# A four-layer graph block on Trainium2: attention's output product from twelve-bit parts in every step, with the transposes in one group and the next block's scores behind the mix

## The chip, the cores and the metric

The kernel runs on one core of a Trainium2 chip. The metric is the device time of one execution in microseconds (us), the median of repeated runs; lower is better. All times below are of this kernel on this chip. PE is the matrix engine, PEld its weight loads, DVE the vector engine, ACT the scalar engine, POOL the GpSimd engine, SP the queue that issues most transfers.

## The reference

`x` holds 1024 nodes by 512 features. After a normalisation and a first graph convolution, four layers follow, and then a second graph convolution and two residual sums. Per layer:

```python
def _attn(xf, cond, Wq, Wk, Wv, Wo):            # BS, M, H, DH = 16, 256, 8, 64
    xb = xf.reshape(BS, n // BS, d)             # 16 batches of 64 nodes
    q = (xb @ Wq).reshape(BS, -1, H, DH)
    k = (cond @ Wk).reshape(BS, -1, H, DH)      # cond: 16 x 256 x 512
    v = (cond @ Wv).reshape(BS, -1, H, DH)
    att = jnp.einsum('bnhd,bmhd->bhnm', q, k) * DH ** (-0.5)
    w = jax.nn.softmax(att, axis=-1)
    o = jnp.einsum('bhnm,bmhd->bnhd', w, v).reshape(BS, -1, H * DH)
    return (o @ Wo).reshape(n, d)
...
for i in range(L):                              # L = 4
    h = h + _attn(_ln(h, ln2_w[i], ln2_b[i]), cond, Wq[i], Wk[i], Wv[i], Wo[i])
    u = _ln(h, ln3_w[i], ln3_b[i]) @ geglu_w[i] + geglu_b[i]
    val, gate = jnp.split(u, 2, axis=-1)
    h = h + (val * jax.nn.gelu(gate, approximate=False)) @ ffo_w[i] + ffo_b[i]
```

The product that the change rewrites is `o @ Wo`, 1024x512 by 512x512, once per layer.

## The kernel before, in words

`h` lives in eight tiles of 128 rows, h[0] to h[7] (`hall` in the trace). Block g holds two batches of 64 nodes. The attention of a layer is a loop over g (L1580 onwards); in **step g** the keys and values of block g+1 are made while the softmax of block g is finished and weighed with its values.

**Twelve-bit products.** Keys and values come from class `Twelve` (L338 to L384). An operand x is cut into a high part (ACT, L314), a low part (DVE, L315) and a third part, high minus low (POOL, L320, in four pieces `as_c` of 128x512 per block). `begin` multiplies high by high and low by low, 4 matmuls of 128x512 each in the fp32r type (L366), and ACT scales the bank in place (L377). `end` adds third by third on top, 4 matmuls, and copies the bank out (DVE L382 or ACT L384). So PE cannot start a unit's `end` before ACT has done that unit's L377. Four units make the keys k_0 to k_3 of a block and four the values v_0 to v_3.

**Softmax.** `scores` issues 32 matmuls (L835), four row maxima on DVE (L842, `nmax`), eight exponentials on ACT (L847) and on DVE four reciprocals and eight scalings (L850, L852). In step g it stands at the head of the step, between v_2's and v_3's `end` of block g. `mix` transposes the four probability tiles on PE (`tr_pr`, L201), copies them out as `pT` (ACT L886 and DVE L884, in turn), and multiplies them with the values, 64 small matmuls into the bank `po` (L870). Between the second and third transposed tile and behind the fourth it calls hooks, in which k_3's `end` and v_0's `begin` are multiplied. DVE copies `po` to `oT` (L893).

**Output product.** Blocks 0 to 5 go by pairs: in every odd step `pair_sums` makes sums of the two `oT` on POOL (L919 to L922) and `attn_out_pair` makes seven products of 2 x 128x256 matmuls per bank half (through `multiply`, L297; tiles `oab`, `ocd`) in plain fp32, spread between the value units and the next step's scores, with sums on DVE and POOL. The right-hand sums `wo_sums` are made once a layer on POOL (L909). Blocks 6 and 7 go alone through `attn_out` (L899, `pw`, plain fp32), in a tail in which the first products of the feed-forward part (`ga`, class `Quad`, L297) fill PE.

**Order.** PE's order is that of the code, held by `pin`. DVE, ACT and POOL are in-order queues, filled by a scheduler that keeps to the readiness it models unless `in_order`, `waiting_for` or `issue_after` say otherwise. In odd steps `split_cond`, which cuts the operand for the block after next, stood behind `pair_sums` by `tc.issue_after`. The base of the last residual sum (`x_again`, `bias_out`) is fetched and added in steps 1 and 2 of each layer (L1557, L1558).

Of the kernel before, what the change touches and what calls it, by code (L numbers as in the profile page):

```python
# [17 lines left out]
P = 128  # L18
# [7 lines left out]
def gnn_kernel(  # L26
# [82 lines left out]
    def bank(name):  # L109
        return psum.tile([P, 512], F32, tag="bank", name=name)  # L110
# [746 lines left out]
    def mix(l, g, probs, v, hooks, each=pin):  # L857

        oT = t512(f"oT_{l}_{g}")
        po = bank(f"po_{l}_{g}")  # L860
# [16 lines left out]
        for c2 in range(2):  # L877
            pTs = []
            for j in range(2):
                u = 2 * c2 + j  # L880
                pt = transposed(probs[u], f"pr_{l}_{g}_{u}", each)
                pT = t512(f"pT_{l}_{g}_{u}")
                if j:
                    nc.vector.tensor_copy(pT, pt)  # L884
# [8 lines left out]
        mix.last = nc.vector.tensor_copy(oT, po)  # L893
        return oT

    def attn_out(l, g, oT, wo):
        pw = bank(f"pw_{l}_{g}")
        for c in range(HP):
            nc.tensor.matmul(pw, oT[:, c * P:(c + 1) * P], wo[c // 2][:, c % 2, :],  # L899
                             start=(c == 0), stop=(c == HP - 1))  # L900
        nc.vector.tensor_tensor(h[g], pw, h[g], OP.add)

    def wo_sums(wo):

        b11, b12, b21, b22 = (wo[k][:, :, d * M:(d + 1) * M] for k in range(2) for d in range(2))
        sums = four_wide("wo_sums")
        t1, t2, t3, t4 = (halves_of(sums[:, i, :]) for i in range(4))
        for to, of, less in ((t1, b12, b11), (t3, b22, b12), (t2, b22, t1), (t4, b21, t2)):
            nc.gpsimd.tensor_tensor(to, of, less, OP.subtract)  # L909
        return [b11, b21, b22, t4, t1, t2, t3]  # L910

    def pair_sums(l, g, oTs):

        n = f"{l}_{g}"
        t = nc.gpsimd
        a11, a12, a21, a22 = (halves_of(oT[:, k * M:(k + 1) * M]) for oT in oTs for k in range(2))
        s, more = acc_tile(f"os_{n}"), acc_tile(f"om_{n}")
        s1, s2, s4 = (halves_of(x) for x in (s[:, :M], s[:, M:], more[:, :M]))
        t.tensor_tensor(s1, a21, a22, OP.add)  # L919
        t.tensor_tensor(a21, a11, a21, OP.subtract)  # L920
        t.tensor_tensor(s2, s1, a11, OP.subtract)
        pair_sums.last = t.tensor_tensor(s4, a12, s2, OP.subtract)  # L922
        return [a11, a12, s4, a22, s1, s2, a21], more[:, M:], acc_tile(f"ou_{n}")

    def attn_out_pair(g, left, p1, kept, right, ab, cd, each=lambda ins: ins):


        t = nc.gpsimd
        a, b, c, d = ab[:, :M], ab[:, M:], cd[:, :M], cd[:, M:]
        h11, h12, h21, h22 = (h[g + i][:, j * M:(j + 1) * M] for i in range(2) for j in range(2))  # L930

        def product(i, to, start):
            multiply(to, left[i], right[i], [(0, P, 0, M)], start, each)

        u2, p7 = kept[:, :M], kept[:, M:]
        product(0, a, True)
        nc.scalar.copy(p1, a)
        product(6, c, True)
        nc.scalar.copy(p7, c)
        yield  # L940
        product(5, b, False)
        nc.vector.tensor_tensor(u2, b, p1, OP.add)
        t.tensor_tensor(p7, p7, u2, OP.add)
        product(4, d, False)
        nc.vector.tensor_tensor(h22, d, h22, OP.add)
        t.tensor_tensor(h22, p7, h22, OP.add)
        yield
        product(1, a, False)
        nc.vector.tensor_tensor(h11, a, h11, OP.add)
        product(3, c, False)  # L950
        nc.vector.tensor_tensor(h21, c, h21, OP.add)
        t.tensor_tensor(h21, u2, h21, OP.add)
        yield
        product(2, d, False)
        nc.vector.tensor_tensor(h12, d, h12, OP.add)
        t.tensor_tensor(h12, u2, h12, OP.add)

# [20 lines left out]
    class Quad:  # L978
# [12 lines left out]
        def first(self):  # L991
            self.a = bank(f"ga_{self.n}")
            self.product(0, self.a, True)
            self.s1 = acc_tile(f"gs1_{self.n}")
            nc.scalar.copy(self.s1, self.a)
# [457 lines left out]
    for l in range(L):  # L1453
# [92 lines left out]
        def fetch_x(nb):  # L1546
            fetched[nb] = acc_tile(f"x_again_{nb}"), acc_tile(f"bias_out_{nb}")
            nc.sync.dma_start(fetched[nb][0], x[nb * P:(nb + 1) * P, :])
            load_row(gcn_out_b, 0, "bias_out", fetched[nb][1])

        def base_of(nb):


            (xt, bias_out), xn = fetched.pop(nb), acc_tile(f"again_{nb}")
            nc.scalar.activation(xn, xt, AF.Relu, bias=x_shift[:, nb:nb + 1],
                                 scale=x_root[:, nb:nb + 1])
            nc.vector.tensor_tensor(xt, xt, bias_out, OP.add)  # L1557
            nc.vector.tensor_tensor(xt, xt, xn, OP.add)  # L1558
            nc.sync.dma_start(base_dram[nb], xt)
# [18 lines left out]

        oTs, ends = [], []
        for g in range(NG - 1):  # L1580
            if g == NG - 2:
                take_ln3()
                raw = load_geglu(l, 0)
                add_bias(nc.vector)
            probs = scores(l, g, qT, kTs.pop(g))
            for end in ends:
                end()
            if g == NG - 2:
                with waiting_for(scores.last, mybir.EngineType.Pool):
                    left = geglu_weights(l, 0, *raw)  # L1590
            if not g:
                with waiting_for(scores.last, mybir.EngineType.Pool):
                    wo7 = wo_sums(wo)
            if g in (1, 2):
                fetch_x(2 * l + g - 1)
            k = keys(l, g + 1, wk, 1 if l == 0 and g == 0 else 0)
            for i, u in enumerate(k):
                u.begin()
                if i > 1:
                    k[i - 2].end()  # L1600
            k[-2].end()
            v = values(l, g + 1, wv)
            with in_order(mybir.EngineType.DVE) if g == NG - 2 else nullcontext():
                oTs.append(mix(l, g, probs, vs.pop(g), (
                    k[-1].end, nothing, lambda: (v[0].begin(), g == NG - 2 and
                                                 add_bias(nc.vector, *range(4))))))
            if g == NG - 2:
# [16 lines left out]
            v[1].end()  # L1624
            if g % 2:
                pair = attn_out_pair(g - 1, *blocks, wo7, bank(f"oab_{l}_{g}"), bank(f"ocd_{l}_{g}"),
                                     pin)
                next(pair)
                if g > 1:
                    moments_into(mv_kept[:, 2 * (g - 3):2 * (g - 1)], [h[g - 3], h[g - 2]],  # L1630
                                 f"ln3_{l}_{g - 3}")
            if g == NG - 2:
                for nb in range(4):
                    ln3_turn(nb, each=pin)
            v[3].begin()
            if g % 2:
                next(pair)
            v[2].end()
            ends = [v[3].end]
            if g % 2:  # L1640
                next(pair)
                ends.insert(0, lambda pair=pair: next(pair, None))
                if g == NG - 3:
                    scale_kept()
            if g == NG - 2:
# [4 lines left out]
            if l == 0 and g + 3 < NG:  # L1650
                turn_cond(g + 3, each=pin)
        oT, = oTs
        g = NG - 1
# [5 lines left out]
        def all_parts():  # L1659
            for i in EARLY:  # L1660
# [10 lines left out]
                for _ in flow:  # L1671
                    yield
            yield

# [9 lines left out]
        with in_order(mybir.EngineType.DVE):  # L1684
            attn_out(l, g - 1, oT, wo)
            fill()
# [6 lines left out]
            add_bias(nc.vector, g - 1)  # L1693
            fill(4)
            attn_out(l, g, oT, wo)
            xns[g], = normalised([h[g]], f"ln3_{l}_{g}")
# [26 lines left out]

        first_chunk = []

        def fill_or_split():
            if next(parts, True) and first_chunk:
                next(first_chunk.pop(0))

        for c, q in enumerate(quads):  # L1730
            if c == 2:
                first_chunk.extend([ready[0].split_steps(False, nc.vector)] * 3 +
                                   [ready[0].split_steps(True, nc.vector)] * 2)
                next(first_chunk[0])
                next(first_chunk[-1])
            q.rest(fill_or_split if c > 1 else fill)
# [252 lines left out]
```

## Time and profile before

| what | us |
|---|---|
| median of 3 runs | 2320.69 (2320.29 to 2322.24) |
| the profiled execution | 2320.22 |
| its span in the trace | 2318.4 |
| PE busy | 2298.9 (99%) |
| DVE busy | 1618.8 (70%) |
| ACT busy | 1080.7 (47%) |
| POOL busy | 741.4 (32%) |
| granted TensorE clock | 1.000 |

The profiled execution's own time and its span differ by 1.8 us, which lie outside of the trace. A row of a timeline gives the start in us from the span's start, the length of the run of like instructions, the engine, the line, the operation, its output and inputs, the shape, how many there are, and in brackets how long the engine stood idle before it and what ended that. Matmuls overlap in the pipe, so the pace of PE is read from the start of one run to the start of the next, not from the durations.

### The profile page before, as it was taken

The numbers are of one execution on the slowest core, as the hardware profiler recorded it, in microseconds if no ns is written. First come the engines' busy times: TensorE is split into PE (matmuls) and PEld (weight loads), VectorE is DVE, ScalarE is ACT, GpSimd is POOL, SyncE is SP. The second block draws the span as 40 slices with busy tenths as digits, with TensorE's granted clock in tenths as the row PEclk, the third lists the DMA queues.
The fourth block names the chain that finished last, engine by engine and source line by source line (L and its number), as shares of the span: only waits on it lengthen the run. The fifth ranks groups of instructions, "written<-read, shape, count | busy, mean of one in ns | idle before, by whom it ended". The sixth has DMA issues, their size and how long they took to land. (4 is left out here: it accounts for less than half of the span.)

```text
span 2318.4 us, 33851 instructions
## 1 busy us (share of the span) xinstructions
PE 2298.9 (99%) x12272; PEld 1715.1 (74%) x12272; DVE 1618.8 (70%) x3060; ACT 1080.7 (47%) x2099; POOL 741.4 (32%) x695
## 2 busy tenths in 40 slices
PE   8999999999999999999999999999999999999999
PEld 4668887577877887477886888577786888667787
DVE  9875457888974546878985445878886544888964
ACT  7544454455244445455344444545334444545410
POOL 1133223373032235175022333266022223246111
PEclk9999999999999999999999999999999999999999
DMA  6052120245411101144521101134531111034550
GB/s 209 11 163 79 55 87 6 69 127 179 153 64 66 45 19 37 51 126 137 181 74 69 61 27 37 35 106 119 182 127 69 42 46 38 5 114 125 176 191 37
DMA packets 161069, 205.43 MB, mean 89 GB/s; under 512 B 11304, under 2 KB 101744, under 8 KB 160896
## 3 DMA queue, kind: packets, MB, share of 16 engines
q1 hardware_dynamic: 158800, 197.77, 26.4%
q0 software_dynamic: 1376, 4.30, 0.5%
q8 instruction: 102, 1.67, 0.3%
q10 hardware_dynamic: 720, 1.11, 0.1%
q14 instruction: 71, 0.58, 0.1%
HBM read 152.80 MB, written 50.34 MB: 88 GB/s over the span
## 5 line engine op out<-in xcount | busy, mean ns | idle before, releaser
L320 POOL TENSOR_TENSOR as_c<-ah_c,al_c 128x512 fp32r<-128x512 f32 x128 | 196.9, 1568 | 409.6 <-PE fy L1265 235.0
L1133 ACT ACTIVATE g<-g 128x512 f32<-128x512 f32 x192 | 112.7, 587 | 193.8 <-PE g L1119 193.8
L377 ACT ACTIVATE v<-v 128x512 f32<-128x512 f32 x127 | 74.1, 584 | 210.4 <-PE v L366 208.3
L1265 PE MATMUL fy<-bh_wff,ah_f 128*128 128x512 f32 x512 | 159.2, 392 | 0.0
L1265 PE MATMUL fx<-bs_wff,as_f 128*128 128x512 f32 x512 | 157.7, 389 | 0.5 <-DVE as_f L317 0.5
L1265 PE MATMUL fy<-bl_wff,al_f 128*128 128x512 f32 x512 | 157.8, 389 | 0.0
L314 ACT ACTIVATE ah_f<-fr 128x1024 fp32r<-128x1024 f32 x64 | 67.6, 1061 | 173.7 <-PE fy L1265 116.4
L366 PE MATMUL v<-bh_wv,ah_c 128*128 128x512 f32 x508 | 145.4, 408 | 0.0
L847 ACT ACTIVATE pr<-sc,nmax 128x256 f32<-128x256 f32 x256 | 118.3, 475 | 53.9 <-DVE nmax L842 53.4
L366 PE MATMUL v<-bs_wv,as_c 128*128 128x512 f32 x508 | 143.4, 404 | 0.0
L377 ACT ACTIVATE k<-k 128x512 f32<-128x512 f32 x125 | 72.7, 585 | 144.1 <-PE k L366 144.1
L366 PE MATMUL v<-bl_wv,al_c 128*128 128x512 f32 x508 | 136.3, 390 | 0.0
L1119 PE MATMUL g<-gr,gsa 128*128 128x512 f32 x384 | 136.2, 436 | 0.0
L1065 POOL TENSOR_TENSOR gsa<-gha,gla 128x512 fp32r<-128x512 f32 x88 | 112.2, 1297 | 70.2 <-DVE gla L1061 69.1
L366 PE MATMUL k<-ah_c,bh_wk 128*128 128x512 f32 x500 | 134.5, 391 | 0.0
L366 PE MATMUL k<-al_c,bl_wk 128*128 128x512 f32 x500 | 133.9, 390 | 0.0
L366 PE MATMUL k<-as_c,bs_wk 128*128 128x512 f32 x500 | 132.1, 395 | 0.0
L1119 PE MATMUL g<-gr,gha 128*128 128x512 f32 x384 | 120.6, 395 | 0.0
L382 DVE COPY kT<-k 128x512 f32<-128x512 f32 x54 | 37.4, 692 | 118.9 <-PE k L366 118.9
L1119 PE MATMUL g<-gl,gla 128*128 128x512 f32 x384 | 118.6, 390 | 0.0
L1265 PEld LDWEIGHTS fy<-bh_wff,ah_f 128*128 128x128 f32 x512 | 96.1, 188 | 21.5 <-issue 1.9
L366 PEld LDWEIGHTS v<-bs_wv,as_c 128*128 128x128 f32 x508 | 93.9, 188 | 24.2 <-issue 4.6
(354 smaller groups left out, 5558.6 us busy)
## 6 DMA issues: line engine op xcount, KB each, us to landing
f_dram<-fT SPq DMA_DIRECT2D x128, 256.0 KB, 2.6
fr<-f_dram SPq DMA_DIRECT2D x64, 512.0 KB, 4.4
ct<-cond_dram SPq DMA_DIRECT2D x48, 512.0 KB, 4.1
wff<-in_L_gnn_ffo_w_dram SPq DMA_DIRECT2D x32, 512.0 KB, 5.8
gxb<-in_L_gnn_geglu_w_dram SPq DMA_DIRECT2D x96, 128.0 KB, 2.7
gxa<-in_L_gnn_geglu_w_dram SPq DMA_DIRECT2D x96, 128.0 KB, 2.6
cond<-in_L_gnn_cond_dram SPq DMA_DIRECT2D x32, 256.0 KB, 3.5
cond_dram<-ct SPq DMA_DIRECT2D x16, 512.0 KB, 3.7
```

The source lines that it names most:

```text
L314: nc.scalar.mul(twelve_bits(h), x, INWARD * TINY)
L320: nc.gpsimd.tensor_tensor(twelve_bits(s)[:, k, :], h[:, k, :], l[:, k, :], OP.subtract)
L366: pin(nc.tensor.matmul(self.bank, twelve_bits(left[k // 2])[:, k % 2, self.c * P:(self.c + 1) * P], twelve_bits(right[k // 2])[:, k % 2, : ...
L377: nc.scalar.mul(self.bank, self.bank, 1.0 + TINY)
L382: nc.vector.tensor_copy(self.to(), self.bank)
L847: nc.scalar.activation(pr3[:, a, :], ps3[:, a, :], AF.Exp, bias=nmax[:, a:a + 1], accum_out=tot[:, a:a + 1])
L1065: split_left.last = pin(t.tensor_tensor(s_at, h_at, l_at, OP.subtract))
L1119: pin(nc.tensor.matmul(to, self.part(i, which)[:, k, :], self.rights[i][which].bitcast(F32R)[:, k, :], start=start and k == 0, stop=stop a ...
L1133: pin(nc.scalar.mul(to, to, 1.0 + TINY))
L1265: pin(nc.tensor.matmul(to, twelve_bits(left[which][0])[:, k, b * P:(b + 1) * P], twelve_bits(right[which])[:, k, :], start=u == 0 and whic ...
```

## The change

`mix` no longer makes a copy of `po` but three parts: `oh` (high, ACT, L893 of the changed kernel), `ol` (low, DVE, L894) and `os` (third, DVE, L895). `attn_out` multiplies them with three parts of Wo, 12 matmuls of 128x512 in fp32r (L903): four high by high and four low by low into one bank `oy`, four third by third into a bank `ox`, and DVE adds both to h[g] (L908, L911). It runs in every step for g = 0 to 5, in three pieces between value units, and in the tail for blocks 6 and 7. `out_parts` cuts Wo once a layer, in step 0 (two ACT operations of 128x1024, two DVE operations of 128x1024 and four of 128x512). `wo_sums`, `pair_sums` and `attn_out_pair` are gone, and `split_cond` no longer stands behind `pair_sums`.

Beside this, the four `tr_pr` of a `mix` stand in one group, with the hooks behind it, and `scores` of block g+1 stands right behind `mix` of block g, for g = 0 to 5. Smaller edits: `bias_out` is fetched once a layer into a tile of its own; the tiles `gs1` of class `Quad` share two slots; in the tail `fill(4)` is gone and the first chunk is split wholly beside the last `Quad`.

```diff
     def mix(l, g, probs, v, hooks, each=pin):
-        oT = t512(f"oT_{l}_{g}")
         po = bank(f"po_{l}_{g}")
...
-            hooks[c2]()
-        hooks[2]()
+        for hook in hooks:
+            hook()
         for c2, pTs in enumerate(turned):
             weigh(c2, pTs)
-        mix.last = nc.vector.tensor_copy(oT, po)
-        return oT
+        parts = high, low, third = [t512(f"o{n}_{l}_{g}") for n in "hls"]
+        nc.scalar.mul(twelve_bits(high), po, INWARD * TINY)
+        nc.vector.scalar_tensor_tensor(twelve_bits(low), high, -1.0 / TINY, po, OP.mult, OP.add)
+        mix.last = nc.vector.tensor_tensor(twelve_bits(third), high, low, OP.subtract)
+        return parts
+
+    def attn_out(l, g, left, right, each=lambda ins: ins):
+        y, x = bank(f"oy_{l}_{g}"), bank(f"ox_{l}_{g}")
+        for which, to in enumerate((y, y, x)):
+            for c in range(HP):
+                each(nc.tensor.matmul(to, twelve_bits(left[which])[:, c * P:(c + 1) * P],
+                                      twelve_bits(right[which][c]),
+                                      start=c == 0 and which != 1, stop=c == HP - 1 and which != 0,
+                                      skip_group_check=True))
+            if which == 1:
+                nc.vector.scalar_tensor_tensor(h[g], y, 1.0 + TINY, h[g], OP.mult, OP.add)
+            if which < 2:
+                yield
+        nc.vector.tensor_tensor(h[g], x, h[g], OP.add)
+
+    def out_parts(l, wo):
+        high = four_wide(f"oh_{l}")
+        low = slots_of(2, f"ol_{l}")
+        third = [acc_tile(f"os_{l}_{c}") for c in range(HP)]
+        for k in range(2):
+            nc.scalar.mul(twelve_bits(high)[:, 2 * k:2 * k + 2, :], wo[k], INWARD / TINY)
+        for k in range(2):
+            of = high[:, 2 * k:2 * k + 2, :]
+            nc.vector.scalar_tensor_tensor(twelve_bits(low[k]), wo[k], 1.0 / TINY, of, OP.mult,
+                                           OP.subtract)
+            for i in range(2):
+                out_parts.last = nc.vector.scalar_tensor_tensor(
+                    twelve_bits(third[2 * k + i]), of[:, i, :], -TINY, low[k][:, i, :], OP.mult,
+                    OP.add)
+        return ([high[:, c, :] for c in range(HP)], [low[c // 2][:, c % 2, :] for c in range(HP)],
+                third)
...
-            probs = scores(l, g, qT, kTs.pop(g))
-            for end in ends:
-                end()
+            if not g:
+                probs = scores(l, g, qT, kTs.pop(g))
...
-                    wo7 = wo_sums(wo)
+                wo = out_parts(l, wo)
             k = keys(l, g + 1, wk, 1 if l == 0 and g == 0 else 0)
             for i, u in enumerate(k):
                 u.begin()
+                if not i:
+                    for end in ends:
+                        end()
                 if i > 1:
                     k[i - 2].end()
             k[-2].end()
...
+            if g < NG - 2:
+                probs = scores(l, g + 1, qT, kTs.pop(g + 1))
...
-            if g % 2:
-                blocks = pair_sums(l, g - 1, oTs)
-                oTs.clear()
-            with tc.issue_after(pair_sums.last.ins) if g % 2 else nullcontext():
-                split_cond(l, g + 2)
+            split_cond(l, g + 2)
             v[1].begin()
             v[0].end()
             v[2].begin()
             v[1].end()
-            if g % 2:
-                pair = attn_out_pair(g - 1, *blocks, wo7, bank(f"oab_{l}_{g}"), bank(f"ocd_{l}_{g}"),
-                                     pin)
-                next(pair)
+            pieces = attn_out(l, g, oT, wo, pin) if g < NG - 2 else iter(())
+            next(pieces, None)
...
             v[3].begin()
-            if g % 2:
-                next(pair)
+            next(pieces, None)
             v[2].end()
+            next(pieces, None)
             ends = [v[3].end]
-            if g % 2:
-                next(pair)
-                ends.insert(0, lambda pair=pair: next(pair, None))
```

Three places show how the order moves, all in layer 1 around the end of step 2. Names are tile_block_unit: `v_3_1` is unit v_1 of block 3, `po_2` the mix of block 2, `sc_3_0` the first score bank of block 3; the number behind is the compiler's.

ACT, from v_0's scale of block 3 on. Before:

```order
L377 ACTIVATE v_3_0_21243<-v_3_0_21243 128x512
L377 ACTIVATE v_3_1_21309<-v_3_1_21309 128x512
L384 COPY v_3_0_21323<-v_3_0_21243 128x512
L377 ACTIVATE v_3_2_21326<-v_3_2_21326 128x512
L377 ACTIVATE v_3_3_21341<-v_3_3_21341 128x512
L384 COPY v_3_1_21324<-v_3_2_21326 128x512
L847 ACTIVATE pr_3_0_21378,tot_3_0_21379<-sc_3_0_21356,nmax_3_0_21376 128x256 x2
```

ACT at the same place, of the change:

```order
L377 ACTIVATE v_3_0_21308<-v_3_0_21308 128x512
L893 ACTIVATE oh_2_21350<-po_2_21274 128x512
L847 ACTIVATE pr_3_0_21378,tot_3_0_21379<-sc_3_0_21356,nmax_3_0_21376 128x256 x2
L847 ACTIVATE pr_3_1_21388,tot_3_1_21389<-sc_3_1_21357,nmax_3_1_21386 128x256 x2
L847 ACTIVATE pr_3_2_21398,tot_3_2_21399<-sc_3_2_21358,nmax_3_2_21396 128x256 x2
L847 ACTIVATE pr_3_3_21408,tot_3_3_21409<-sc_3_3_21359,nmax_3_3_21406 128x256 x2
L377 ACTIVATE v_3_1_21439<-v_3_1_21439 128x512
L384 COPY v_3_0_21453<-v_3_0_21308 128x512
L377 ACTIVATE v_3_2_21456<-v_3_2_21456 128x512
```

The high part and all eight exponentials of block 3 now stand ahead of v_1's scale; before they stood behind the scales of all four value units.

DVE, around the end of `mix` of block 2. Before:

```order
L315 SCALAR_TENSOR_TENSOR al_c_4_1_21294<-ah_c_4_1_21292,ct_4_1_21005 128x1024
L893 COPY oT_2_21208<-po_2_21209 128x512
L382 COPY v_3_0_21323<-v_3_1_21309 128x512
L842 TENSOR_REDUCE nmax_3_0_21376<-sc_3_0_21356 128x2
L842 TENSOR_REDUCE nmax_3_1_21386<-sc_3_1_21357 128x2
```

DVE at the same place, of the change:

```order
L315 SCALAR_TENSOR_TENSOR al_c_4_1_21424<-ah_c_4_1_21422,ct_4_1_21144 128x1024
L894 SCALAR_TENSOR_TENSOR ol_2_21351<-oh_2_21350,po_2_21274 128x512
L895 TENSOR_TENSOR os_2_21352<-oh_2_21350,ol_2_21351 128x512
L842 TENSOR_REDUCE nmax_3_0_21376<-sc_3_0_21356 128x2
L842 TENSOR_REDUCE nmax_3_1_21386<-sc_3_1_21357 128x2
L842 TENSOR_REDUCE nmax_3_2_21396<-sc_3_2_21358 128x2
L850 RECIPROCAL inv_3_0_21382<-tot_3_0_21379 128x2
```

Low and third part stand ahead of the first row maximum.

PE, from the last matmuls of the scores to the second piece of the output product, of the change (before, v_1's `begin` followed on `po`, and the scores of block 3 came behind v_2's `end`):

```order
L835 MATMUL sc_3_3_21359<-kT_3_1_21252,qT_0_1_20494 64x256 x2
L366 MATMUL v_3_1_21439<-bh_wv_0_0_20154,ah_c_3_0_21129 128x512 x2
L366 MATMUL v_3_1_21439<-bh_wv_1_0_20194,ah_c_3_1_21130 128x512 x2
L366 MATMUL v_3_1_21439<-bl_wv_0_0_20155,al_c_3_0_21131 128x512 x2
L366 MATMUL v_3_1_21439<-bl_wv_1_0_20195,al_c_3_1_21132 128x512 x2
L366 MATMUL v_3_0_21308<-bs_wv_0_0_20156,as_c_3_0_21133 128x512 x2
L366 MATMUL v_3_0_21308<-bs_wv_1_0_20196,as_c_3_1_21134 128x512 x2
L366 MATMUL v_3_2_21456<-bh_wv_0_0_20154,ah_c_3_0_21129 128x512 x2
L366 MATMUL v_3_2_21456<-bh_wv_1_0_20194,ah_c_3_1_21130 128x512 x2
L366 MATMUL v_3_2_21456<-bl_wv_0_0_20155,al_c_3_0_21131 128x512 x2
L366 MATMUL v_3_2_21456<-bl_wv_1_0_20195,al_c_3_1_21132 128x512 x2
L366 MATMUL v_3_1_21439<-bs_wv_0_0_20156,as_c_3_0_21133 128x512 x2
```

Between the last score matmul and v_1's `end` (its rows with `bs_wv`, which need v_1's scale on ACT) stand 20 matmuls of 128x512.

More of the change, by code (lines that the diff above doesn't have):

```diff
@@ L903, in wo_sums @@
[L903 to L956, printed above, removed]
+        parts = high, low, third = [t512(f"o{n}_{l}_{g}") for n in "hls"]
@@ L1577, in nothing @@
             pass
-        oTs, ends = [], []
+        ends = []
         for g in range(NG - 1):
@@ L1684, in gnn_kernel @@
         with in_order(mybir.EngineType.DVE):
-            attn_out(l, g - 1, oT, wo)
+            for _ in attn_out(l, g - 1, oT, wo):
+                pass
             fill()
@@ L1693, in gnn_kernel @@
             add_bias(nc.vector, g - 1)
[L1694 to L1695 removed]
+            for _ in attn_out(l, g, oT, wo):
+                pass
             xns[g], = normalised([h[g]], f"ln3_{l}_{g}")
@@ L1722, in split, with split_first @@
                 ready[n].split(low, t)
[L1724 to L1728, printed above, removed]
-        for c, q in enumerate(quads):
[L1731 to L1736, printed above, removed]
+        def split_first():
+            long, short = (ready[0].split_steps(low, nc.vector) for low in (False, True))
+            next(long)
+            next(short)
+            return [parts] + [long] * 3 + [short] * 2
+        for c, q in enumerate(quads):
+            if c == KC - 1:
+                first_chunk = split_first()
+            q.rest((lambda: next(first_chunk.pop(0), None)) if c == KC - 1 else fill)
             if c == 0:
```

37 lines of the change are left out of this document (16 added, 21 removed).

## The prediction

> **What bounds the kernel now.** I read the page's busy times first, then what PE waits for, then PE's timeline through layer 1. From the page:
>
> ```profile
> PE 2298.9 (99%) x12272; PEld 1715.1 (74%) x12272; DVE 1618.8 (70%) x3060; ACT 1080.7 (47%) x2099; POOL 741.4 (32%) x695
> ```
>
> and the first of PE's own waits, longest total first (us in total, times, longest):
>
> ```profile
> PE edges L485 <- DVE edges_f L472: 3.9, 1, 3.9
> ```
>
> PE is busy 99% of the span, and its longest wait is a single one of 3.9 us for the edges at the program's start. So inside the layers each us of PE work removed is a us won, each one added is lost, and **any new wait of PE is paid in full**. That cuts both ways: the other engines do not matter until one of them is late for PE, and then it matters at once. PE's runs in layer 1, from a mix to the one after next:
>
> ```profile
> 719.29 2.08 PE L870 MATMUL po<-pT,v 128*64 128x64 f32 x64
> 721.30 1.20 PE L366 MATMUL v<-bh_wv,ah_c 128*128 128x512 f32 x4
> 722.34 1.07 PE L366 MATMUL v<-bl_wv,al_c 128*128 128x512 f32 x4
> 723.25 1.07 PE L366 MATMUL v<-bs_wv,as_c 128*128 128x512 f32 x4
> 724.16 1.07 PE L366 MATMUL v<-bh_wv,ah_c 128*128 128x512 f32 x4
> ...
> 728.69 1.07 PE L366 MATMUL v<-bs_wv,as_c 128*128 128x512 f32 x4
> 729.69 1.96 PE L835 MATMUL sc<-kT,qT 64*64 64x256 f32 x32
> 731.58 1.21 PE L366 MATMUL v<-bs_wv,as_c 128*128 128x512 f32 x4
> 732.62 1.09 PE L366 MATMUL k<-ah_c,bh_wk 128*128 128x512 f32 x4
> ...
> 747.25 2.08 PE L870 MATMUL po<-pT,v 128*64 128x64 f32 x64
> ...
> 781.27 2.08 PE L870 MATMUL po<-pT,v 128*64 128x64 f32 x64
> ```
>
> Three readings. Four fp32r matmuls of 128x512 take 0.907 us (723.25 to 724.16), 0.227 each. Where the kind of matmul changes, a little is lost: the run at 728.69 takes 1.00, those at 721.30 and 731.58 take 1.04, so 0.09 to 0.13 over 0.907. And mix to mix is 27.96 us without and 34.02 us with a pair's product (747.25 - 719.29, 781.27 - 747.25): the product of a pair costs 6.06 us, **3.03 us a block**.
>
> **The work on PE, part by part.** The new product is 12 x 0.227 = 2.72 us a block, so -0.31 us a step. The scores leave their place between two value units (loss 0.09 ahead and 0.13 behind) and stand behind `po`, where a change of kind stood anyway: about -0.22. Putting the four transposes together takes out one change of kind of about 0.1 and makes one run of 16; I set it at -0.02, between 0 and -0.1. Together **-0.55 us a step**, 6 steps in 4 layers: 24 x -0.55 = -13.2 us. In the tail, blocks 6 and 7 go alone in plain fp32:
>
> ```profile
> 921.19 3.60 PE L899 MATMUL pw<-wo,oT 128*128 128x512 f32 x8
> 924.62 3.60 PE L297 MATMUL ga<-ln3T,wval 128*128 128x512 f32 x8
> ```
>
> That is 3.43 us each (924.62 - 921.19), against 2.72: -0.71, eight times, -5.7 us. If nothing waits, the profiled execution goes from 2320.2 to **2301.3 us**.
>
> **The wait that comes in.** In the new order ACT meets, behind the mix, the high part, then eight exponentials of the next block, and only then the scale of v_1; PE needs that scale for v_1's third product. The exponentials need the row maxima, and these stand on DVE behind the low and the third part. Count from the moment at which PE leaves `po` (721.30 in the rows above; call it 0). The links, from the trace:
>
> ```profile
> 721.42 0.69 DVE L893 COPY oT<-po 128x512 f32<-128x512 f32 x1 [0.35 <-PE po L870]
> ...
> 730.82 1.29 DVE L842 TENSOR_REDUCE nmax<-sc 128x2 f32<-128x512 f32 x2 [3.05 <-PE sc L835]
> ```
>
> ```profile
> 731.54 0.48 ACT L847 ACTIVATE pr<-sc,nmax 128x256 f32<-128x256 f32 x1 [1.16 <-DVE nmax L842]
> ...
> 735.48 0.60 ACT L377 ACTIVATE k<-k 128x512 f32<-128x512 f32 x1
> ```
>
> ```profile
> 704.71 0.48 ACT L847 ACTIVATE pr<-sc,nmax 128x256 f32<-128x256 f32 x1 [0.39 <-DVE nmax L842]
> ...
> 708.32 1.12 ACT L377 ACTIVATE k<-k 128x512 f32<-128x512 f32 x2
> ```
>
> ```profile
> L377 ACT ACTIVATE v<-v 128x512 f32<-128x512 f32 x127 | 74.1, 584 | 210.4 <-PE v L366 208.3
> ```
>
> ```profile
> L1272 DVE SCALAR_TENSOR_TENSOR hall<-fy,hall 128x512 f32<-128x512 f32 x32 | 21.9, 683 | 14.8 <-PE fy L1265 14.8
> ```
>
> ```profile
> 703.39 0.68 DVE L1557 TENSOR_TENSOR x_again<-x_again,bias_out 128x512 f32<-128x512 f32 x1
> 703.99 1.28 DVE L842 TENSOR_REDUCE nmax<-sc 128x2 f32<-128x512 f32 x2
> ```
>
> - High starts 0.12 behind `po` (721.42 - 721.30) and takes 0.58 as L377 does, the nearest row, also an ACT scaling of a PSUM bank: done at 0.70.
> - Low: handed over in some 0.05, and 0.68 as L1272, which also reads one operand from PSUM: 0.75 to 1.43.
> - Third starts at about 1.46; the next operation follows 0.60 behind its start, as behind L1557 (703.99 - 703.39), a two-input operation of that size: the first maximum starts at about 2.07.
> - From its start to the first exponential 0.72 (731.54 - 730.82): 2.79. Eight exponentials with their reads of the sums: 3.61 (708.32 - 704.71): v_1's scale starts at 6.40 and, with 0.58 and a handover of 0.05, PE can have it at **7.03**.
>
> PE in that time: scores 1.89 (731.58 - 729.69), v_1's `begin` 1.04 + 0.91, v_0's `end` 0.91, v_2's `begin` 1.81, in all 6.56. So PE stands for **0.47 us** in each of the 24 steps even if every link is at its best. Before, the scales of all four units stood ahead of the exponentials, and the trace shows no such wait.
>
> One link will not be at its best. `as_c` of the block after next runs on POOL at that time, and in its company a DVE operation with two SBUF inputs is longer:
>
> ```profile
> 717.35 1.22 DVE L315 SCALAR_TENSOR_TENSOR al_c<-ah_c,ct 128x1024 fp32r<-128x1024 f32 x1
> ...
> 719.09 1.99 DVE L315 SCALAR_TENSOR_TENSOR al_c<-ah_c,ct 128x1024 fp32r<-128x1024 f32 x1
> ```
>
> ```profile
> 718.71 6.01 POOL L320 TENSOR_TENSOR as_c<-ah_c,al_c 128x512 fp32r<-128x512 f32 x4 [3.44 <-DVE al_c L315]
> ```
>
> ```profile
> 712.61 2.66 POOL L909 TENSOR_TENSOR wo_sums<-wo,wo_sums 128x512 f32<-128x512 f32 x2
> ```
>
> The second `al_c` took 0.77 us more than the first. A POOL operation of a piece's size takes some 1.3 us (2.66 for two), and when that `al_c` started 718.71 + 1.3 - 719.09 = 0.9 us of the first piece was left, so it looks as if DVE waited for the piece. The four pieces lasted from -2.6 to 3.4 on my count, and they are released by the same `al_c` as before, so the third part (both inputs in SBUF) starts in the middle of them. Ends: 0 if it falls between two pieces, and 1.3 if it meets a whole one. Counting the pieces forward from the `al_c` of the new order, one of them ends about 0.5 behind the third part's turn; I take **+0.5**. The low part reads `po` from PSUM, as `oT` did at 721.42 beside the same pieces in its usual 0.69, so I add nothing to it. PE then stands for 0.47 + 0.5 = 0.97 us, and a step is -0.55 + 0.97 = **+0.42 us**: 24 x 0.42 = +10.1 us.
>
> The Trainium skill bears on that link: "SBUF — State Buffer", section "SBUF: two separate sides", states that DVE and GpSimd share a port pair as an exclusive lock, for a DVE operation with two SBUF inputs against a GpSimd operation that reads SBUF, held for the whole instruction. By that rule the third part waits for the rest of the running piece, which gives the sum of 10 us; if every meeting cost the flat 0.77 of the second `al_c`, the step would be +0.69 and the sum 17 us. The rows above (0.77 lost with 0.9 left) lean to the rule without proving it.
>
> **Smaller terms.** In step 0 of each layer `out_parts` puts 2 x 1.22 + 4 x 0.69 us on DVE and 2 x 1.06 us on ACT beside the first softmax, two of the DVE pieces inside it. Its exponentials end at 708.32 and k_0's scale follows, while PE comes to k_0's third product here:
>
> ```profile
> 710.14 1.07 PE L366 MATMUL k<-as_c,bs_wk 128*128 128x512 f32 x4
> ```
>
> The scale could end at 708.90, so 1.2 us are free and two pieces of 0.69 take 1.4: a stall of about 0.2. The two additions of `x_again` (0.68 each) fall behind block 0's softmax now and can put off the low part by some 0.5. Together +0.7 a layer, +3 us; ends 0 and 1.2 a layer. The four POOL operations of `wo_sums` and the POOL sums of the pairs cost nothing now and give nothing, since PE waits for none of them.
>
> In the tail, block 7's mix needs its `pT` from DVE, and DVE comes to it at 930.36, behind the normalisation of block 6, while PE takes up `po` at 931.62:
>
> ```profile
> 930.36 1.28 DVE L884 COPY pT<-tr_pr 128x512 f32<-128x512 f32 x2
> ```
>
> ```profile
> 931.62 2.09 PE L870 MATMUL po<-pT,v 128*64 128x64 f32 x64
> ```
>
> The new product ends in two additions on DVE in place of one, so this chain gets 0.6 later while PE gets 0.7 earlier: the gain of block 6 is eaten by a wait for `pT`. Of block 7 I keep 0.5 a layer: -2 us in place of -5.7.
>
> **Sum.** 2320.2 + 10.1 + 3 - 2 = 2331.3 us. The profiled execution lies 0.5 us below the median of the runs; I forecast **2331 us**.
>
> **Rivals.**
> - *The exponentials come in time.* For: the count of 7.03 against 6.56 is a difference of two sums of ten terms. Against: each link has a row, and none of them can be left out. Without any stall a step is -0.55, and with the smaller terms half as large the time is 2320.2 - 13.2 - 4 + 1 = **2304 us**. It decides if the chain is shorter by over 0.5 us. This is also the case in which the change does what it says and nothing else. Chance 0.12.
> - *The stall is there, without POOL's part.* Then a step is -0.55 + 0.47 = -0.08: -2 us, and with +2 and -2 for the rest **2318 us**. It needs the third part to fall between two pieces of `as_c`, or these to run later than I count. Chance 0.23.
> - *More stall.* The third part meets a whole piece (1.3), and the exponentials go at the pace of the run that waits for a maximum in its middle, 3.94 us (731.54 to the next scale at 735.48) in place of 3.61. The stall is 0.47 + 1.3 + 0.33 = 2.1, a step is +1.55, and the time 2320.2 + 37 + 1 = **2358 us**; half-way 2345. Chance 0.15.
> - *The new matmuls are not at 0.227 us.* Each needs a weight load; those of the same form take 188 ns and lie beside a matmul in this trace:
>
> ```profile
> L366 PEld LDWEIGHTS v<-bs_wv,as_c 128*128 128x128 f32 x508 | 93.9, 188 | 24.2 <-issue 4.6
> ```
>
> Were a load not hidden, 12 x 32 x 0.188 = 72 us would come on top. The value units run in this form at 0.907 for four, so I give it 0.01 and leave it out of the range.
>
> **How the numbers follow.** Forecast 0.49, rivals 0.12, 0.23, 0.15 and 0.01. A measurement of this kernel tells 0.2% (4.6 us) from no change, so 2316.0 to 2325.3 counts as the same. The forecast's own range is 2324 to 2341 (the third part's wait 0.2 to 0.9 us). The range that should hold the time 8 times in 10 takes in the second rival and half of the third: 2312 to 2347. Faster: the first rival and a small part of the second, 0.17. Same: most of the second and the forecast's edge, 0.21. Slower: 0.62.
>
> **What would show it.** In PE's waits, a new row for v's third product (`bs_wv`) waiting for ACT's scale of v, about 24 times, 0.5 to 1 us each, 20 to 25 us in all. In a step's timeline, 12 matmuls `oy` and `ox` in 2.7 to 2.8 us; mix to mix about 31.4 us in every step instead of 27.96 and 34.02; the third part longer than 0.69 us and beside an `as_c`; the first exponential 3.2 us behind `po`. Wrong would be: no wait at v_1's `end` (then the first rival), a wait elsewhere of the same size (the chain that I followed is not the last one), or a step without waits longer than 30.5 us.

## The result, and the profile after

The changed kernel takes **2347.93 us** (median of 4 runs, 2347.0 to 2348.61), beside 2320.49 for the kernel before in the same comparison: a ratio of 1.0118 with a 95% interval of 1.0105 to 1.013. It is slower by 27.4 us. The forecast was 2331 us, with a range up to 2347: the direction was right, the size was not. The profiled execution took 2347.34 us with a span of 2345.6, which is 27.2 more than before.

Busy times of the changed kernel, from its page, and the first two of PE's waits inside the layers:

```profile
PE 2296.0 (98%) x12256; PEld 1715.3 (73%) x12256; DVE 1690.7 (72%) x3112; ACT 1086.9 (46%) x2115; POOL 658.7 (28%) x583
```

```profile
PE v L366 <- ACT v L377: 24.2, 24, 2.2
PE g L1094 <- ACT g L1108: 5.7, 4, 1.4
```

Before, PE waited for nothing in the layers but a few tenths. Now there are two new long waits: 24 times (six steps in four layers) for ACT's scale of a value unit, at most 2.2 us, and once a layer for ACT's scale of a product `g` in the feed-forward part. A step of layer 1 on PE, from one mix to the next:

```profile
758.70 2.08 PE L869 MATMUL po<-pT,v 128*64 128x64 f32 x64
760.72 1.96 PE L835 MATMUL sc<-kT,qT 64*64 64x256 f32 x32
...
766.37 1.07 PE L366 MATMUL v<-bl_wv,al_c 128*128 128x512 f32 x4
768.23 1.21 PE L366 MATMUL v<-bs_wv,as_c 128*128 128x512 f32 x4 [0.79 <-ACT v L377]
769.28 1.08 PE L903 MATMUL oy<-oh,oh 128*128 128x512 f32 x4
...
790.29 2.09 PE L869 MATMUL po<-pT,v 128*64 128x64 f32 x64
```

The step takes 31.59 us (790.29 - 758.70) against 30.99 on average before. The run at 766.37 would take 0.907 us and takes 1.86: PE stands for 0.95 us, and the run behind the wait needs 1.05 instead of 0.91, 0.14 for starting again. What PE waited for, in the next step, on DVE, POOL and ACT (PE left `po` at 792.30):

```profile
793.05 0.69 DVE L894 SCALAR_TENSOR_TENSOR ol<-oh,po 128x512 fp32r<-128x512 f32 x1 [1.09 <-ACT oh L893]
793.77 1.10 DVE L895 TENSOR_TENSOR os<-oh,ol 128x512 fp32r<-128x512 f32 x1
794.80 1.87 DVE L842 TENSOR_REDUCE nmax<-sc 128x2 f32<-128x512 f32 x3
```

```profile
789.60 6.42 POOL L320 TENSOR_TENSOR as_c<-ah_c,al_c 128x512 fp32r<-128x512 f32 x4 [25.16 <-issue]
```

```profile
792.42 0.60 ACT L893 ACTIVATE oh<-po 128x512 fp32r<-128x512 f32 x1 [1.38 <-PE po L869]
795.51 0.47 ACT L847 ACTIVATE pr<-sc,nmax 128x256 f32<-128x256 f32 x1 [2.50 <-DVE nmax L842]
...
799.12 0.63 ACT L377 ACTIVATE v<-v 128x512 f32<-128x512 f32 x1
```

This is the chain of the forecast link by link: high 0.12 behind `po`, low at 0.75, third at 1.47 and 1.10 long beside POOL's pieces, the first maximum at 2.50, the first exponential at 3.21, the scale 3.61 later. But step 0 of a layer is worse. In layer 2, on DVE and PE:

```profile
1267.03 1.49 DVE L1534 TENSOR_TENSOR x_again<-x_again,bias_out 128x512 f32<-128x512 f32 x1
1268.44 2.29 DVE L315 SCALAR_TENSOR_TENSOR al_c<-ah_c,ct 128x1024 fp32r<-128x1024 f32 x1
1270.66 0.68 DVE L1535 TENSOR_TENSOR x_again<-x_again,again 128x512 f32<-128x512 f32 x1
1271.26 0.67 DVE L894 SCALAR_TENSOR_TENSOR ol<-oh,po 128x512 fp32r<-128x512 f32 x1
```

```profile
1277.97 1.83 PE L366 MATMUL v<-bs_wv,as_c 128*128 128x512 f32 x4 [1.89 <-ACT v L377]
1279.60 1.91 PE L903 MATMUL oy<-oh,oh 128*128 128x512 f32 x4
1281.30 1.27 PE L366 MATMUL v<-bh_wv,ah_c 128*128 128x512 f32 x4
```

```profile
1277.97:1279.60 1.63, 1.63 (x5) 1.29 (x6) 0.31 (x2) 0.95 (x2) 0.00 (x0) 0.60 0.00 0
1279.60:1281.30 1.70, 1.70 (x5) 1.32 (x4) 0.69 (x1) 0.00 (x0) 0.00 (x0) 0.50 0.00 0
```

(The last fence is a table by stretches: behind the comma stands PE's busy time, and the third number from the end is the granted clock of TensorE.) PE left `po` at 1269.36, the high part was there at 1270.08, and the low part started only at 1271.26: DVE was still at an addition for `x_again` and an `al_c`, both drawn out beside POOL. So the wait is 1.89 us, and behind it the clock is granted at about half: the next eight matmuls take 3.33 us instead of 1.81. In the feed-forward part of layer 1, on DVE, POOL, ACT and PE in the order of cause:

```profile
995.32 0.69 DVE L1040 TENSOR_TENSOR gsb<-ghb,glb 128x512 fp32r<-128x512 f32 x1
```

```profile
996.15 0.74 POOL L1074 TENSOR_TENSOR gxa<-gxa,gxb 128x256 f32<-128x256 f32 x1 [19.75 <-DVE gsb L1040]
```

```profile
998.43 1.06 ACT L1034 ACTIVATE gha<-gxa 128x1024 fp32r<-128x1024 f32 x1 [1.93 <-POOL gxa L1074]
999.40 0.58 ACT L1108 ACTIVATE g<-g 128x512 f32<-128x512 f32 x1
```

```profile
1000.03 0.73 PE L1094 MATMUL g<-gr,gsa 128*128 128x512 f32 x2 [1.43 <-ACT g L1108]
```

The split of the first chunk, which the change moved wholly beside the last `Quad`, ends at 996.0. POOL's sums for the second chunk are held until then (`waiting_for(split_left.last)` in the code, 19.75 us of idle POOL in the row), ACT's high part of that chunk waits for the sums, and the scale that PE needs stands behind it on ACT.

A shorter wait stands inside block 7's mix, behind its first two matmuls, for a `pT` that DVE reaches behind the product's two additions and block 6's normalisation. On DVE and PE in layer 1:

```profile
938.62 0.68 DVE L911 TENSOR_TENSOR hall<-ox,hall 128x512 f32<-128x512 f32 x1
...
942.29 1.28 DVE L883 COPY pT<-tr_pr 128x512 f32<-128x512 f32 x2
```

```profile
942.40 0.33 PE L869 MATMUL po<-pT,v 128*64 128x64 f32 x2
943.03 2.08 PE L869 MATMUL po<-pT,v 128*64 128x64 f32 x62 [0.30 <-DVE pT L883]
945.04 1.12 PE L297 MATMUL ga<-ln3T,wval 128*128 128x512 f32 x2
```

That mix takes 2.64 us (945.04 - 942.40) instead of 2.01, so 0.63 more, though PE's list of waits has only 0.30 of it.

Where the 27 us are, from the starts of `po` in the two traces (us a layer; steps 1 to 5 as their mean; in layer 3 the fourth row goes to the second graph convolution):

| stretch | layer 0 | layer 1 | layer 2 | layer 3 |
|---|---|---|---|---|
| a step before, mean of the six | 32.43 | 30.99 | 30.99 | 30.99 |
| step 0, after | 34.72 | 32.65 | 34.22 | 34.21 |
| steps 1 to 5, after | 33.02 | 31.60 | 31.59 | 31.59 |
| last mix to the next layer's scores, after less before | +1.79 | +1.65 | +1.74 | +1.72 |
| block 6's mix to block 7's, after less before | -0.66 | -0.66 | -0.66 | -0.66 |

### The profile page after: what moved, and what is told of

It is laid out like the page before. It is cut to its first block, busy times and chain, and to the rows that moved or that the text cites. A ratio compares the mean times of both kernels' runs of the same rounds, so it can differ in the third digit from the quotient of the medians.

```text
span 2345.6 us, 33610 instructions
## 1 busy us (share of the span) xinstructions
PE 2296.0 (98%) x12256; PEld 1715.3 (73%) x12256; DVE 1690.7 (72%) x3112; ACT 1086.9 (46%) x2115; POOL 658.7 (28%) x583
## 3 DMA queue, kind: packets, MB, share of 16 engines
q8 instruction: 101, 1.65, 0.3%
q10 hardware_dynamic: 720, 1.11, 0.1%
## 5 line engine op out<-in xcount | busy, mean ns | idle before, releaser
L320 POOL TENSOR_TENSOR as_c<-ah_c,al_c 128x512 fp32r<-128x512 f32 x128 | 211.8, 1684 | 938.5 <-DVE al_c L315 569.6
L1036 DVE SCALAR_TENSOR_TENSOR gla<-gha,gxa 128x1024 fp32r<-128x1024 f32 x48 | 82.1, 1710 | 46.1 <-ACT gha L1034 41.5
```

Of the source, the lines that this page charges most:

```text
L320: nc.gpsimd.tensor_tensor(twelve_bits(s)[:, k, :], h[:, k, :], l[:, k, :], OP.subtract)
L1036: pin(nc.vector.scalar_tensor_tensor(l.bitcast(F32R), h, -1.0 / TINY, x, OP.mult, OP.add))
```

## The experiments

The theory after the result: three separate costs. PE waits for v_1's scale behind the exponentials in 24 steps; in step 0 the `x_again` additions make that wait longer, and the clock drops behind some of them; and the held sums make PE wait in the feed-forward part. The rival: DVE, at 72%, is short as a whole, and a wait taken away turns up elsewhere. Each edit is against the changed kernel if nothing else is said. The ratio is to the kernel before, beside which each was run.

**a_v1_first**

```diff
-            if g < NG - 2:
-                probs = scores(l, g + 1, qT, kTs.pop(g + 1))
...
             v[1].begin()
+            if g < NG - 2:
+                probs = scores(l, g + 1, qT, kTs.pop(g + 1))
             v[0].end()
```

> The changed kernel with one move: the scores of the next block stand behind v_1's begin, so that v_1's scale is ahead of the exponentials on ACT. Theory (the order on ACT makes PE wait at v_1's third product: 24 waits of 28 us together, 3 us for starting again, and 3 us of half clock behind two of them): all of it goes, less some 2 us for one more change of kind on PE: 2316 us, and no row of v waiting for ACT. Rival (DVE is the engine that is short, the wait is only where it shows): the wait turns up at another unit and the time stays above 2340 us.

Measured: 2318.4 us, ratio 0.9991 (0.9982 to 1.0001). All waits for v's scale are gone; the wait for `g` remains and is the first of PE's list:

```profile
PE g L1094 <- ACT g L1108: 5.6, 4, 1.4
```

Every step takes 30.72 us in layers 1 to 3, step 0 too. DVE did the same work, so it is not short as a whole: the rival falls for these 24 waits. The move costs changes of kind of matmul, since the scores stand between two value units again: 30.72 a step, where i_split_exps below, with the scores left behind `po`, has 30.46.

**b_third_late**

```diff
-        mix.last = nc.vector.tensor_tensor(twelve_bits(third), high, low, OP.subtract)
...
             if g < NG - 2:
                 probs = scores(l, g + 1, qT, kTs.pop(g + 1))
+                mix.last = behind_scores(nc.vector.tensor_tensor(
+                    twelve_bits(oT[2]), oT[0], oT[1], OP.subtract))
```

(`behind_scores` orders an operation behind the last scaling of the softmax on DVE; the mix of blocks 6 and 7 keeps its third part.)

> The changed kernel with the third part of the mix (L895) behind the softmax of the next block on DVE, ACT's order untouched. Theory (the chain is high, low, third, first maximum, eight exponentials, scale, and the third part holds 1.03 us of it): the steady wait of 0.97 us goes to about 0, that of step 0 from 2.05 to 1.0, the half clock goes: about 2319 us. Rival (ACT's order alone makes the wait, the exponentials are too long in any case): at most 0.3 us a step, 2340 us or more.

Measured: 2325.25 us, ratio 1.002 (1.001 to 1.003). ACT's order is as in the changed kernel, and of the 24 waits PE's list has four left, those of step 0:

```profile
PE v L366 <- ACT v L377: 5.3, 4, 2.1
```

Steps 1 to 5 go to 30.71 us. That is still 0.25 above i_split_exps below, whose order on PE is the same: 0.10 us is lost ahead of v_1's third product, too short for the list, and 0.12 in the run behind it. So the third part makes 0.85 of the 0.95 us of wait, and ACT's order alone only the rest. Over the expectation of 2319 us stand these 20 steps, 5 us together, and step 0. In layers 1 to 3 its wait fell by 0.79, not by a whole third part (the step takes 31.87 us); in layer 0 it stayed at 2.1, and the step takes 36.19, where the matmuls behind the wait have a pace of 0.42 us: there the clock drops.

**g_no_meet**

```diff
-            split_cond(l, g + 2)
+            with waiting_for(mix.last, mybir.EngineType.Pool):
+                split_cond(l, g + 2)
```

> The changed kernel with POOL's pieces as_c held until the third part of the mix is done, so that the two never meet. Theory (the third part loses 0.4 us to the pieces in every step, on the chain that PE waits for): the third part takes 0.69, the steady wait 0.97 - 0.41 = 0.56 us, about 10 us less: 2338 us. Rival (it is long by itself, as an fp32r operation that reads what the one ahead has just written): it stays at 1.1 us, 2347 us.

Measured: 2329.51 us, ratio 1.0039 (1.0025 to 1.0053). The third part (minimum, median, maximum in ns) and the waits:

```profile
L895 DVE TENSOR_TENSOR os<-oh,ol x32: 691/692/694, 179.0 to 2014.2; 128x512 fp32r<-128x512 f32 x32
```

```profile
PE v L366 <- ACT v L377: 9.2, 24, 0.4
```

Kept apart from POOL's pieces the third part takes 0.69 us in all 32 cases, and a step goes from 31.59 to 31.16: 0.43 us, the 0.41 by which the third part got shorter. The rest of the gain, over the 10 us expected, is step 0, where `al_c` and `x_again` no longer meet POOL either.

**d_x_late**

```diff
-            nc.vector.tensor_tensor(xt, xt, bias_out, OP.add)
-            nc.vector.tensor_tensor(xt, xt, xn, OP.add)
+            behind_scores(nc.vector.tensor_tensor(xt, xt, bias_out, OP.add))
+            behind_scores(nc.vector.tensor_tensor(xt, xt, xn, OP.add))
```

> The changed kernel with the two additions of x_again held behind the softmax of the next block on DVE. Theory (two of them and a longer al_c put off the low part of step 0, the wait there is 2.05 us instead of 0.97, and behind it in layers 2 and 3 the matrix clock is granted at half for 3 us): 4 x 1.1 + 2 x 1.6 = 7.6 us less, 2340 us, and the clock at 1.00 behind the wait of step 0. Rival (step 0 is longer for the parts of Wo or the first softmax): 2346 us or more.

Measured: 2340.11 us, ratio 1.0084 (1.0067 to 1.0101), as the theory had it. No drop of the clock is left in the layers. The longest wait for v's scale falls from 2.2 to 1.2 us, and step 0 of layers 1 to 3 takes 31.6 us like the others:

```profile
PE v L366 <- ACT v L377: 20.3, 24, 1.2
```

**c_tail_back**

```diff
+            yield
         parts = all_parts()
...
             add_bias(nc.vector, g - 1)
+            fill(4)
             for _ in attn_out(l, g, oT, wo):
...
-            if c == KC - 1:
-                first_chunk = split_first()
-            q.rest((lambda: next(first_chunk.pop(0), None)) if c == KC - 1 else fill)
+            if c == 2:
+                first_chunk.extend([ready[0].split_steps(False, nc.vector)] * 3 +
+                                   [ready[0].split_steps(True, nc.vector)] * 2)
+                next(first_chunk[0])
+                next(first_chunk[-1])
+            q.rest(fill_or_split if c > 1 else fill)
```

> The changed kernel with the tail's filling and the split of the first chunk as they were before (the four steps of fill, the fill ahead of block 7's product, the split beside the last two quads). Theory (the later split puts off POOL's sums for the second chunk, ACT's high part of that chunk waits for them, and the scale of the first chunk's fourth product stands behind it on ACT: 1.43 us and the restart in each layer): 6.7 us less, 2341 us, and no row of g waiting for ACT g. Rival (that wait comes from the product's additions on DVE, or its saving is eaten in block 7's normalisation): 2346 us or more.

Measured: 2352.42 us, ratio 1.0138 (1.0121 to 1.0155), slower than the changed kernel: the expectation missed, the rival's second half held. The wait for `g` is gone, and a longer one stands in the tail:

```profile
PE v L366 <- ACT v L377: 24.3, 24, 2.2
PE gb L297 <- DVE ln3S L234: 8.1, 4, 2.0
```

The steps of `fill` stand on DVE ahead of block 7's two additions (from 951.67 to 954.08 in layer 1), and with them its normalisation and the sums `ln3S` come too late. The edits of the tail in the change are thus not idle: with the new product DVE cannot do this work there. They moved the price to the other end. On balance the old tail costs some 0.5 us a layer more; the rest of the difference between the two traces is three more drops of the clock, behind step 0's wait in layers 0 and 1 and in layer 2's tail.

**h_sum_early**, against a_v1_first:

```diff
-        with waiting_for(split_left.last, mybir.EngineType.Pool):
-            sum_chunk(1)
+        sum_chunk(1)
```

> As a_v1_first (scores behind v_1's begin), and POOL's sums for the second chunk of the feed-forward part no longer held behind the split of the first chunk. Theory (that hold, with the split made later, is what makes PE wait for ACT's g scale for 1.4 us a layer): 6.7 us under a_v1_first, 2311.7 us, no such wait. Rival (the sums beside the split cost DVE as much, or the scale is late for another reason): 2316 to 2320 us.

Measured: 2312.64 us, ratio 0.9965 (0.9953 to 0.9978), 5.8 us under a_v1_first. No long wait for `g` is left in PE's list, and the stretch from the last mix to the next layer's scores is what it was before, within 0.1 us. That is 1.6 to 1.7 us a layer less than in a_v1_first and 6.7 in all, as expected. The medians differ by less, but the profiled execution of h_sum_early, at 2313.97 us, lost 2.2 us ahead of the layers, where its clock is at half from 86.2 to 89.6 us (first mix at 177.62 against 175.40). The hold was the cause of the wait.

**e_old_place**

```diff
-            if not g:
-                probs = scores(l, g, qT, kTs.pop(g))
+            probs = scores(l, g, qT, kTs.pop(g))
+            for end in ends:
+                end()
...
-            if g < NG - 2:
-                probs = scores(l, g + 1, qT, kTs.pop(g + 1))
```

> The changed kernel with the scores back at the head of the next step, where they were before; the product from parts, the grouped transposes and the tail stay. Theory (the waits come from the moved scores, and the product alone saves 3.03 - 2.79 = 0.24 us a block): no wait for v's scale, about 30.73 us a step, 2319 to 2320 us. Rival (the parts of the mix on ACT and DVE cost waits of their own at any place): above 2325 us with a new wait in PE's list.

Measured: 2317.46 us, ratio 0.9988 (0.9978 to 0.9998). A step takes 30.67 us, and no wait for v's scale is left. The third part is still long here (median 1134 ns) but nothing waits for it. So the parts of the mix cost PE nothing by themselves: product and grouping alone save 0.32 us a step, and it is the scores' new place that turns them into a wait.

**i_split_exps**

```diff
     for u in range(4):
+            if u == 2 and between:
+                scaled = between()
...
+                if scaled is not None:
+                    tc.add_manual_dep(ex.ins, scaled.ins.name, ...)
...
-                probs = scores(l, g + 1, qT, kTs.pop(g + 1))
+                probs = scores(l, g + 1, qT, kTs.pop(g + 1), v[1].begin)
```

> The changed kernel with PE's order untouched, and v_1's scale put between the fourth and the fifth exponential on ACT. Theory (only the place of the scale behind all eight exponentials makes PE wait; four of them end 5.0 us behind po, the scale 0.6 later, and PE comes at 6.56): no wait, about 30.49 us a step, step 0 at most 0.2 more: 2314 us. Rival (the later exponentials then hold up the scale of v_2 or the softmax of the block): a wait at v_2's third product or at the transposes, 2325 us or more.

Measured: 2315.05 us, ratio 0.9979 (0.9969 to 0.9988). PE's order is that of the changed kernel, v_1's scale stands behind four exponentials, and steps 1 to 5 of layers 1 to 3 take 30.46 us, 0.53 under the mean before. No wait at v_2 or at the transposes turned up. Step 0 takes 30.83 there, and in layer 0 33.59 against 32.21 in its steps 1 to 4, where one wait is left:

```profile
PE v L366 <- ACT v L377: 1.1, 1, 1.1
```

In step 0 the `x_again` additions still stand ahead of the low part; j_all_three below moves them too, and this wait goes.

**j_all_three**: the edits of i_split_exps, d_x_late and h_sum_early together.

> The three edits that took away a wait, together: v_1's scale between the exponentials (i_split_exps), x_again's additions behind the softmax (d_x_late), POOL's sums not held (h_sum_early). Theory (three separate costs that add up): 2315 us of i_split_exps, less 5.8 for the sums, less 0.37 in step 0 of three layers and 1.4 in that of layer 0: about 2307 us. Rival (they share slack on DVE, so that one uncovers another): 2310 to 2315 us.

Measured: **2305.49 us**, ratio 0.9934 (0.992 to 0.9947), faster than both kernels. Steps 0 to 5 take 30.46 us each in layers 1 to 3, and PE's list begins with the wait at the program's start, as before the change. The three costs add up.

## Why the prediction was wrong in size

- **Work on PE: right.** Forecast -0.55 us a step without waits; with PE's order unchanged and the wait removed it is -0.53 (30.46 against 30.99). Forecast without any wait 2301.3 us, measured 2305.49 with all three removed; 3 us of the rest are the tail, below.
- **The wait for v_1's scale: right, place and size.** Forecast 0.97 us in 24 steps; 0.95 in the steady ones. That the chain decides was shown from three sides: its last link moved (a, i), one link taken out (b), one link shortened by 0.41 and the step by 0.43 (g). The rule of the Trainium skill ("SBUF — State Buffer", section "SBUF: two separate sides") on the shared port pair fits: the third part took 0.41 us more beside POOL and nothing more without, and the last section has 64 cases in which the loss followed what was left of the running piece and was no flat 0.77. The forecast had taken 0.5 for that rest; it was 0.55 in the step shown. What the sum lacked is for the most part the restart behind the wait, 0.14 us: a steady step is +0.61, not +0.42, and 24 steps make +4.5 us more.
- **Step 0: the step that was mis-sized.** "The two additions of `x_again` (0.68 each) ... can put off the low part by some 0.5. Together +0.7 a layer, +3 us." One of them and an `al_c` fell just ahead of the low part and each met POOL's pieces (1.49 and 2.29 us instead of 0.68 and 1.22), so that the low part started 1.2 us late; and in layers 2 and 3 the clock drop cost 1.5 us more. Step 0 is 1.4, 1.1, 2.6 and 2.6 us over the steps that follow (in layer 0 over its steps 1 to 4, 33.37 on average), 7.7 us; with 0.2 us ahead of the first mix in three layers about 8 us in place of 3. d_x_late took away 7.8.
- **The feed-forward part: the step that failed.** The sum of the prediction goes up to block 7 and has no term behind it: the later split of the first chunk was not costed, and what waits for its end was not looked up. It is POOL's hold, then ACT's queue, then PE: 1.65 to 1.79 us a layer, 6.9 us in all, of which h_sum_early gave back 6.7 in the traces.
- **The tail: right.** Forecast: block 6's gain eaten by a wait for `pT`, 0.5 a layer kept of block 7. The wait is there, inside block 7's mix, which takes 0.63 longer. From block 6's mix to the end of block 7's product PE is 0.70 us faster (layer 1), so 0.70 is kept. In the table the row of blocks 6 and 7 ends where block 7's mix starts: its -0.66 is block 6's gain, and in the row above it block 7's gain and the wait for `pT` cancel.

Together: 11.1 of the forecast's sum (10.1 + 3 - 2), +4.5 for the steady steps, +5 for step 0, +6.9 for the feed-forward part, -0.6 for the tail make 26.9 of the 27.2 us.

## What to carry to other kernels

On an engine that never waits, a saving of 0.5 us a step is worth less than the order of the in-order queue that feeds it: look for the operation that the full engine needs and count what now stands ahead of it there. A wait costs more than its length, because the engine loses time starting again and, where too much of the wait falls into one cell of the grid described below, its clock. And follow every moved block of work to its last reader, here POOL's held sums and an ACT operation behind them, also where the diff looks like housekeeping.

## What the runs showed of the hardware that was not expected

Behind some of the long waits TensorE ran at half clock, a loss of some 1.5 us. In the traces the granted clock changes only on a grid of 3.413 us, and each drop inside the program lasts one cell of it. In the changed kernel and the nine experiments eight such drops lie in the layers and the part behind them. In the cell ahead of each PE was busy for 1.24 to 1.53 of the 3.41 us; in every cell there with no drop behind it PE was busy for 1.64 us or more. So the length of a gap decides only in part. Take a gap from the start of the last matmul ahead of a wait to the start of the first one behind: 96 gaps of 1.15 to 1.82 us were followed by no drop, and of 13 gaps of 2.27 to 2.63 us eight were. What else decides is how the gap lies on the grid. The wait of step 0 in layer 1 makes a gap of 2.27 us in the changed kernel and in c_tail_back. In the changed kernel a boundary of the grid cuts it in two, and the clock stays:

```profile
732.16:735.57 3.41, 2.62 (x12) 1.85 (x10) 3.34 (x12) 3.20 (x15) 0.73 (x1) 1.00 0.33 127
735.57:738.99 3.42, 2.32 (x10) 1.94 (x11) 2.06 (x6) 2.05 (x7) 0.00 (x0) 1.00 0.00 0
738.99:742.40 3.41, 3.41 (x17) 2.79 (x16) 0.69 (x1) 0.58 (x1) 0.00 (x0) 1.00 0.00 0
```

In c_tail_back it lies in one cell, and the next cell is at half:

```profile
735.91:739.32 3.41, 1.53 (x8) 0.93 (x7) 2.77 (x12) 3.41 (x13) 0.00 (x0) 1.00 0.00 0
739.32:742.73 3.41, 3.41 (x10) 2.64 (x9) 0.69 (x1) 0.10 (x1) 0.00 (x0) 0.50 0.00 0
```

Ahead of the layers one cell of the changed kernel with 1.51 us had no drop behind it, so the exact bound stays open. The Trainium skill, "TensorE: Matmul & The Clock Gate", section "HAM oscillation — how this bites in real kernels", warns of idle gaps over about 3.4 us; here shorter ones were enough.

The meeting of DVE and POOL can be counted. In the changed kernel, from the first layer on, 64 DVE operations with both inputs in SBUF started while a piece of `as_c` ran: 24 third parts, 24 `al_c`, four additions of `x_again`, six `al_f` and six `as_f`. Each took longer than it does alone by what was left of the piece at its start, less 0.13 to 0.15 us; that made 0.38 to 1.11 us. The 48 row maxima that started beside a piece, with their input in PSUM, took 0.67 to 0.68 as they do alone. POOL lost as well: in the step of layer 1 above the four pieces took 6.42 us in place of the 5.1 that g_no_meet shows for them (two pairs of 2.54 and 2.58). The second, beside an `al_c`, took 2.25 us and the fourth, beside the third part, 1.74, where one alone takes 1.28.
